# An attention and feed-forward kernel: order of the first loads, weight products side by side, and the place of h1's copies

## Chip, core and metric

The kernel runs on one core of a Trainium2 chip, in float32 (with matmuls in a reduced 32-bit form, written as a high and a low part). The metric is the device time of one execution in microseconds. The median of three runs before the change is 877.68 us (877.13 to 878.19).

## What is computed

The input x has two sequences of 2048 rows and 256 features. The reference, cut to what matters:

```python
xn = _layernorm(x, axis=-1)
q, k, v = xn @ Wq, xn @ Wk, xn @ Wv
attn = softmax(causal(q @ k.T) * 256 ** -0.5)
a = (attn @ v) @ Wo
h = silu((xn @ w1.T) * w1_s) * ((xn @ w2.T) * w2_s)
h = gelu((h @ h1.T) * h1_s)
h = gelu((h @ h2.T) * h2_s)
out = x + a + (h @ w3.T) * w3_s
```

The hidden width is 1024, and w1, w2, h1, h2 and w3 hold only −1, 0 and 1.

## The kernel before

There are two stages. The first, some 280 us, is attention; the second is the feed-forward part (FFN), which begins only when the first has ended and a flag has been read.

**Attention.** Rows are taken in eight blocks of 512 (four to a sequence), each of four tiles of 128 rows. Two algebraic steps shorten the work: Wq and Wk are multiplied into one matrix `wqk`, and Wv and Wo into `wvo`, both by `weights_product` (L217), which makes a high part and a low part of each product. So the keys are just the transposed, normalised x. `keys(n)` (L293) takes one block: `start_keys` (L275) computes mean and variance on VectorE (DVE; `stats`, L235), the root on ScalarE (ACT) and its reciprocal on DVE (`root`, L241), and normalises four tiles on GpSimd (POOL, L283). TensorE (PE) transposes the result (L309), and `hi_lo` (L212) copies it out: the high part on ACT (L214), the low part on DVE (L215). `queries` (L313) multiplies keys by `wqk`, six matmuls of 512 columns for each half; `values` (L327) multiplies keys by `wvo`, 24 matmuls of 256 columns for a block; `score` (L349) multiplies queries by keys. Every such product is a sum of three terms, high by high, high by low and low by high. Softmax exponentials are on ACT (L385). Most of the exponential blocks are transposed through DRAM: DVE turns 32 by 32 squares (L255), one DMA writes them (`d<-b`, L260) and four read them back rearranged (`e<-d`, L267); ACT and DVE or POOL then make the high and low parts `pT` (L423, L425), and `weigh` (L434) multiplies them by the values.

**Beside it.** The kernel chooses a short FFN if all weights are whole, small numbers. It looks at every weight for that: `items` lists pieces of weights of 512 KB or twice 512 KB, which are fetched into `stg` tiles (`fetched_weights`, L577, on ACT's DMA queue) and looked at by DVE, ACT and POOL. w1 and w2 are also rounded into their tiles on the way (`item_low`, L548). For h1, sums of its quarters are written to DRAM (`item_factors`, L554; sums at L150, stored at L541), and three plain quarters are copied from DRAM to DRAM (`copy_factors`, L543): 12 DMAs of 256 KB in all. A planner (`beside`, L600) counts matmul columns and takes the next step of this list, `looks`, when its gap is reached, from the fourth tile on.

**What sets the order.** The program text gives priorities; a scheduler that simulates the engines places each instruction on its engine in the order in which it becomes ready, unless it is tied. `tc.issue_after(ins)` ties what the block issues on that instruction's engine to come after it; it adds no wait. `marks["DVE"]` and `marks["ACT"]` are the latest score scan and the latest exponential. DMAs are started by the instruction queues of SyncE (SP) and of ACT. A DMA that depends on nothing may be placed at the very beginning, and so the h1 copies are: all 12 start between 1.7 and 19.9 us.

**The start.** x's last block of the first sequence is loaded on SP in two halves (L180), Wq and Wk on ACT's queue (L187), then the other blocks on SP. 14 matmuls of zeros (L210) run meanwhile. Wv and Wo are loaded (L611) into the same two tiles after Wq and Wk have been used, and their product stands in the program after the first score. The lines that order it are L608 to L622.

Of the kernel before, what the change touches and what calls it, by code (L numbers as in the profile page):

```python
# [20 lines left out]
P = 128  # L21
TB = 512
# [12 lines left out]
WARM = 14  # L35
# [27 lines left out]
def attn_ffn_kernel(  # L63
# [58 lines left out]
    HK = HC // 2  # L122
    factors = {k: dram.tile([P, len(STEPS), HK, HB], F32, name=f"factors_{k}") for k in ("h1", "h2")}

# [33 lines left out]
    with ExitStack() as actx:  # L158
# [15 lines left out]
        xs, rstds, ks, qs, vs = {}, {}, {}, {}, {}  # L174

        def load_x(n):
            t = xp.tile([P, NT, D], F32, tag="x", name=f"x_{n}")
            for h in range(2):
                src = x[n // NB, ds((n % NB) * TB + h * 2 * P, 2 * P), :]
                nc.sync.dma_start(out=t[:, ts(h, 2), :], in_=src.rearrange("(t p) d -> p t d", p=P))  # L180
            return t

        xs[NB - 1] = load_x(NB - 1)
        raw = {}
        for name, src in (("q", wqT), ("k", wkT)):
            raw[name] = stgp.tile([P, DC, D], F32, tag="stg", name=f"raw_{name}")
            nc.scalar.dma_start(out=raw[name], in_=src)  # L187
        nc.scalar.preload_act_table(AF.Sqrt)
        for n in range(NB - 2, -1, -1):
            xs[n] = load_x(n)  # L190
# [15 lines left out]
        idle = sp.tile([P, S], F32, tag="s", name="idle")[:, : TB // 2].bitcast(BF16)  # L206
        nc.vector.memset(idle, 0.0)
        ps_idle = ps_s.tile([P, TB], F32, tag="ps", name="ps_idle")
        for _ in range(WARM):
            nc.tensor.matmul(out=ps_idle, lhsT=idle[:, :P], rhs=idle, start=True, stop=True)  # L210

        def hi_lo(hi, lo, src):  # L212

            nc.scalar.copy(hi, src)  # L214
            nc.vector.tensor_tensor(lo, src, hi.bitcast(F32), ALU.subtract)  # L215

        def weights_product(name, aT, b, factor):  # L217

            r = cp.tile([P, DC, 2, D], F32R, name=name)
            for c in range(DC):  # L220
                ps = ps_s.tile([P, TB], F32, tag="ps", name=f"ps_{name}_{c}")
                for d in range(DC):
                    nc.tensor.matmul(
                        out=ps[:, :D], lhsT=aT[:, d, ts(c, P)], rhs=b[:, d, :],
                        start=(d == 0), stop=(d == DC - 1),
                    )
                f = rp.tile([P, D], F32, tag="y", name=f"wf_{name}_{c}")
                nc.scalar.mul(f, ps[:, :D], factor)
                nc.vector.tensor_copy(r[:, c, 0, :], f)
                nc.vector.tensor_tensor(  # L230
                    r[:, c, 1, :], f, r[:, c, 0, :].bitcast(F32), ALU.subtract
                )
            return r
# [41 lines left out]
        def start_keys(n):  # L275
            xt = xs.pop(n)
            if n not in rstds:
                mv = cp.tile([P, NT, 2], F32, name=f"mv_{n}")
                stats(xt, mv, n)
                rstds[n] = root(mv, NT, str(n))  # L280
            rstd, off = rstds[n]
            for t in range(NT):
                nc.gpsimd.tensor_scalar(  # L283
# [817 lines left out]
```

## Time and profile before

| what | value |
|---|---|
| median of three runs | 877.68 us |
| the profiled execution | 877.43 us |
| its span | 875.6 us |
| keys, scores and values of the first sequence: last matmul before PE's next wait | ends at 38.68 us |
| first matmul of the FFN (L741) | 279.72 us |
| h1 copies (L544, L546), from issue to landing, least / median / greatest | 3.6 / 5.8 / 7.0 us |
| statistics, DVE L238 and L239, one of each | 0.414 and 0.165 us |
| high part ACT L214, low part DVE L215, 512 columns | 0.587 and about 0.69 us |

The span runs from the first instruction to the last; the rest of the profiled execution, 1.8 us, lies around it. In the lines that follow, PE is the matmul and PEld the loading of its weights. PE's durations overlap, so its pace is read from the time that a group of them takes. A bracket at the end of a line gives the idle time of the engine before it and what ended it. The granted clock (PEclk) is a share of full speed.

### The profile page before, as it was taken

The page shows a single profiled execution, that of the slowest core. Times are in us where ns is not written, and L with a number is a line of the kernel's source. Part 1 is how long each engine was busy: PE and PEld are TensorE (multiplying, and loading weights), DVE is VectorE, ACT ScalarE, POOL GpSimd, SP SyncE. Part 2 cuts the span into 40 slices and gives each one's busy share as a digit, 9 for nine tenths or more (in the row PEclk, how much of TensorE's full clock was granted, in tenths as well). Part 3 has the DMA queues.
Part 4 walks back from the last instruction along what each step waited for, and adds up shares of the span by engine and source line. Part 5 has one row for each costly group of instructions (what it writes and reads, how often), then busy time and mean ns, then how long its engine had stood idle before and what let it go on. Part 6 is the DMA issues. An engine that isn't in the chain of part 4 may idle for free.

```text
span 875.6 us, 12225 instructions
## 1 busy us (share of the span) xinstructions
PE 854.3 (98%) x4280; PEld 721.6 (82%) x4280; DVE 630.6 (72%) x1127; ACT 498.0 (57%) x881; POOL 235.6 (27%) x176
## 2 busy tenths in 40 slices
PE   8999999999998999999999999999999999999996
PEld 5888878988877877888988888888888898888886
DVE  5698689796873995985496596569468648848663
ACT  2546555754753664677266586536557635657670
POOL 4012533202121574440143050025024012502401
PEclk8999999999999999999999999999999999999998
DMA  8877599866892969744424444432434442144312
GB/s 305 326 229 242 168 321 293 302 236 200 238 325 91 365 239 378 258 147 145 139 90 146 147 144 145 156 125 99 144 144 145 147 142 97 49 144 145 144 49 77
DMA packets 63989, 162.51 MB, mean 186 GB/s; under 512 B 6704, under 2 KB 36528, under 8 KB 54704
## 3 DMA queue, kind: packets, MB, share of 16 engines
q1 hardware_dynamic: 58448, 145.92, 48.6%
q10 hardware_dynamic: 5472, 15.73, 5.6%
q8 instruction: 36, 0.59, 0.3%
q14 instruction: 33, 0.27, 0.1%
HBM read 117.06 MB, written 47.71 MB: 188 GB/s over the span
## 4 chain that ended last, share of the span: by engine, by line
PE 70%; DMA 13%; DVE 7%; issue 2%; ACT 2%; SPq 2%; POOL 2%; ACTq 0%; DVEq 0%; POOLq 0%
PE ps_h_X L789 26%; PE ps_w_B L741 13%; PE ps_h_Z L789 13%; PE ps_h_Y L789 7%; PE ps_y L897 6%; DMA e<-d 6%; DMA d<-b 4%; DMA stg<-in_ffn_h_w 2%; SPq L267 2%; DVE b L255 2%; PE pv L336 1%; PE po L443 1%; DVE stg L530 1%; POOL x L283 1%; DVE s L373 1%
## 5 line engine op out<-in xcount | busy, mean ns | idle before, releaser
L364 PE MATMUL pss<-k,q 128*128 128x512 f32 (+3 forms) x480 | 111.0, 369 | 3.1 <-DVE q L215 1.7
L364 PEld LDWEIGHTS pss<-k,q 128*128 128x128 f32 x480 | 81.8, 189 | 16.2 <-DVE q L215 2.1
L789 PE MATMUL ps_h_X<-h_h_T,w_h_S 128*128 128x512 f32 x384 | 89.0, 389 | 0.0
L789 PEld LDWEIGHTS ps_h_X<-h_h_T,w_h_S 128*128 128x128 f32 x384 | 72.1, 188 | 15.0
L443 PE MATMUL po<-v,pT 128*128 128x512 f32 x272 | 79.7, 405 | 3.0 <-ACT pT L423 1.9
L425 POOL TENSOR_TENSOR pT<-e,pT 128x512 fp32r<-128x512 f32 (+3 forms) x30 | 36.3, 1212 | 162.3 <-ACT pT L423 101.6
L887 POOL TENSOR_TENSOR rt<-rt,xt 128x1024 f32<-128x1024 f32 x8 | 19.7, 2458 | 216.5 <-DMA rt<-r_d 200.3
L810 ACT ACTIVATE k_h_u<-k_h_u,h_s_sb 128x512 f32<-128x512 f32 x64 | 46.1, 722 | 41.6 <-DVE k_h_u L809 41.4
L746 ACT ACTIVATE f_w_B<-ps_w_B,w_s_sb 128x512 f32<-128x512 f32 x64 | 42.8, 683 | 43.1 <-PE ps_w_B L741 43.1
L741 PE MATMUL ps_w_B<-xh,w_sb 128*128 128x512 f32 x256 | 60.0, 391 | 2.9 <-DVE f_w_B L747 1.6
L897 PEld LDWEIGHTS ps_y<-w_sbt,h_h_B 128*128 128x128 f32 x512 | 62.0, 192 | 0.3
L897 PE MATMUL ps_y<-w_sbt,h_h_B 128*128 128x256 f32 x512 | 62.1, 283 | 0.0
L423 ACT CAST pT<-e 128x512 fp32r<-128x512 f32 (+3 forms) x60 | 32.6, 573 | 49.6 <-DMA e<-d 38.3
L741 PE MATMUL ps_w_B<-xh1t,w_sb 128*128 128x512 f32 x256 | 60.6, 396 | 0.0
L789 PE MATMUL ps_h_Y<-h_h_B,w_h_A 128*128 128x512 f32 x256 | 59.3, 389 | 0.0
L789 PE MATMUL ps_h_X<-h_h_T,w_h_A 128*128 128x512 f32 x256 | 59.3, 389 | 0.0
L741 PEld LDWEIGHTS ps_w_B<-xh,w_sb 128*128 128x128 f32 x256 | 47.7, 188 | 13.4 <-DVE f_w_B L747 2.0
L443 PEld LDWEIGHTS po<-v,pT 128*128 128x128 f32 x272 | 49.0, 193 | 11.0 <-ACT pT L423 2.4
L741 PEld LDWEIGHTS ps_w_B<-xh1t,w_sb 128*128 128x128 f32 x256 | 48.1, 188 | 11.8
L789 PEld LDWEIGHTS ps_h_Y<-h_h_B,w_h_A 128*128 128x128 f32 x256 | 48.0, 188 | 10.0
L789 PEld LDWEIGHTS ps_h_X<-h_h_T,w_h_A 128*128 128x128 f32 x256 | 48.0, 188 | 10.0
L385 ACT ACTIVATE s<-s,low 128x1024 f32<-128x1024 f32 (+7 forms) x48 | 43.0, 898 | 21.3 <-DVE low L379 21.0
(139 smaller groups left out, 1845.3 us busy)
## 6 DMA issues: line engine op xcount, KB each, us to landing
w_h_S<-factors_h SPq DMA_DIRECT2D x32, 1024.0 KB, 4.7
w_h_A<-factors_h SPq DMA_DIRECT2D x24, 1024.0 KB, 4.7
d<-b SPq DMA_DIRECT2D x18, 512.0 KB, 4.3
e<-d SPq DMA_DIRECT2D x72, 128.0 KB, 4.1
xT_d<-k SPq DMA_DIRECT2D x8, 1024.0 KB, 8.7
stg<-in_ffn_h_w ACTq DMA_DIRECT2D x16, 512.0 KB, 6.5
x<-in_attn_x SPq DMA_DIRECT2D x16, 256.0 KB, 6.5
r_d<-r SPq DMA_DIRECT2D x8, 512.0 KB, 5.5
```

Of the source, the lines that this page charges most:

```text
L255: nc.vector.transpose(b.rearrange("p (g k q) -> p k g q", g=P // Q, q=Q), src.rearrange("p (k g q) -> p k g q", g=P // Q, q=Q),)
L364: nc.tensor.matmul(out=ps[:, :w], lhsT=qs[n][:, c, a, ts(t, P)], rhs=ks[m][:, c, b, :w], start=(k == 0), stop=(m < n and k == 3 * DC - 1),)
L385: marks["ACT"] = nc.scalar.activation(st["s"][:, at], st["s"][:, at], AF.Exp, bias=low, accum_out=st["sums"][:, u // UK : u // UK + 1],).ins
L423: nc.scalar.copy(hi, src)
L425: engine.tensor_tensor(lo, src, hi.bitcast(F32), ALU.subtract)
L443: nc.tensor.matmul(out=st["po"], lhsT=pT[:, 0, ts(j, P)], rhs=vs[m][:, j, :, :], start=(m == first and j == 0), stop=False,)
L741: nc.tensor.matmul(out=p, lhsT=w[:, c, ts(o, P)], rhs=xh[:, c, a, :], start=(c == 0 and a == 0), stop=(c == DC - 1 and a == 1),)
L746: nc.scalar.activation(f, p1, AF.Silu, scale=sc["w1"][:, o : o + 1])
L789: nc.tensor.matmul(out=out[o], lhsT=w[:, c, ts(o, P)], rhs=sets[right][c][:, a, :], start=(start and c == 0 and a == 0), stop=(c == HK - 1 ...
L810: nc.scalar.activation(C[k][o], r[o] if r else banks[o], AF.Gelu, scale=s[:, at : at + 1])
L887: nc.gpsimd.tensor_tensor(rest, rest, xt, ALU.add)
L897: nc.tensor.matmul(out=ys[t][:, :D], lhsT=h[c][:, a, ts(t, P)], rhs=w3_sb[:, c, :], start=(c == 0 and a == 0), stop=(c == HC - 1 and a == 1),)
```

## The change

Its parts:

- x's last block goes out first, one half on SP and one on ACT; then Wq and Wv on SP, Wk and Wo on ACT. Wv and Wo have a tile of their own (from the pool of the turned blocks), so they no longer wait for Wq and Wk. The other x blocks follow on SP.
- `weights_product` makes both halves of a product in one PSUM tile and returns a function that copies them out, 512 columns to an instruction. The product of Wv and Wo stands right after that of Wq and Wk; its copies come after the high and low parts of the first queries.
- The first block's xn is made by POOL (tiles 0 and 2) and ACT (tiles 1 and 3). The statistics of the three next blocks stand behind the low part of `wqk` on DVE.
- The idle matmuls are 26 of 256 columns instead of 14 of 512, and six more follow the first keys.
- In `queries` and `score` the terms are ordered by kind (high by high for both chunks, then low by high, then high by low) instead of by chunk.
- The h1 copies are steps of the w1 and w2 items, 5,000 columns after the look at each, no longer the last step of h1's items; they, and the fetches of the weights that are looked at, are placed behind the latest exponential on ACT.

```diff
-WARM = 14
+WARM = 26
+WARM_KEYS = 6
...
-        def load_x(n):
+        def load_x(n, queues):
             t = xp.tile([P, NT, D], F32, tag="x", name=f"x_{n}")
-            for h in range(2):
+            for h, queue in enumerate(queues):
...
-                nc.sync.dma_start(out=t[:, ts(h, 2), :], in_=src.rearrange("(t p) d -> p t d", p=P))
+                queue.dma_start(out=t[:, ts(h, 2), :], in_=src.rearrange("(t p) d -> p t d", p=P))
...
-        xs[NB - 1] = load_x(NB - 1)
-        raw = {}
-        for name, src in (("q", wqT), ("k", wkT)):
-            raw[name] = stgp.tile([P, DC, D], F32, tag="stg", name=f"raw_{name}")
-            nc.scalar.dma_start(out=raw[name], in_=src)
+        xs[NB - 1] = load_x(NB - 1, (nc.sync, nc.scalar))
+        raw = {name: stgp.tile([P, DC, D], F32, tag="stg", name=f"raw_{name}") for name in "qk"}
+        both = bp.tile([P, 2, DC, D], F32, tag="b", name="raw_vo")
+        raw["v"], raw["o"] = both[:, 0], both[:, 1]
+        for name, src, queue in (
+            ("q", wqT, nc.sync), ("k", wkT, nc.scalar), ("v", wvT, nc.sync), ("o", wo, nc.scalar)
+        ):
+            queue.dma_start(out=raw[name], in_=src)
         nc.scalar.preload_act_table(AF.Sqrt)
         for n in range(NB - 2, -1, -1):
-            xs[n] = load_x(n)
+            xs[n] = load_x(n, (nc.sync, nc.sync))
...
+        def keep_warm(k):
+            for _ in range(k):
+                nc.tensor.matmul(
+                    out=ps_idle[:, : TB // 2], lhsT=idle[:, :P], rhs=idle[:, : TB // 2], start=True, stop=True
+                )
+
+        keep_warm(WARM)
...
+            ps = ps_s.tile([P, DC, D], F32, tag="ps", name=f"ps_{name}")
             for c in range(DC):
-                ps = ps_s.tile([P, TB], F32, tag="ps", name=f"ps_{name}_{c}")
                 for d in range(DC):
...
-                        out=ps[:, :D], lhsT=aT[:, d, ts(c, P)], rhs=b[:, d, :],
+                        out=ps[:, c, :], lhsT=aT[:, d, ts(c, P)], rhs=b[:, d, :],
...
+            def copied():
+                f = rp.tile([P, NT, D], F32, tag="r", name=f"wf_{name}")[:, :DC, :]
+                nc.scalar.mul(f, ps, factor)
+                nc.vector.tensor_copy(r[:, :, 0, :], f)
+                marks["lo"] = nc.vector.tensor_tensor(
+                    r[:, :, 1, :], f, r[:, :, 0, :].bitcast(F32), ALU.subtract
+                ).ins
+
+            return r, copied
...
-                stats(xt, mv, n)
+                with ExitStack() as behind:
+                    if n < NB - 1:
+                        behind.enter_context(tc.issue_after(first_lo))
+                    stats(xt, mv, n)
...
+                if n == NB - 1 and t % 2:
+                    nc.scalar.activation(
+                        xt[:, t, :], xt[:, t, :], AF.Identity,
+                        scale=rstd[:, t : t + 1], bias=off[:, t : t + 1],
+                    )
+                    continue
...
-            for c in range(DC):
-                for a, b in ((0, 0), (0, 1), (1, 0)):
+            for a, b in ((0, 0), (1, 0), (0, 1)):
+                for c in range(DC):
...
         def copy_factors(src, f, c):
-            nc.scalar.dma_start(out=f[:, 0, c, :], in_=src[:, c, :HB])
-            for i in range(2):
-                nc.scalar.dma_start(out=f[:, 5 + i, c, :], in_=src[:, c + HK, ts(i, HB)])
...
+            with tc.issue_after(marks["ACT"]):
+                nc.scalar.dma_start(out=f[:, 0, c, :], in_=src[:, c, :HB])
+                for i in range(2):
+                    nc.scalar.dma_start(out=f[:, 5 + i, c, :], in_=src[:, c + HK, ts(i, HB)])
...
-                (3000, lambda t: copy_factors(src, f, c)),
...
+            copy = (5000, lambda t, c=c: copy_factors(h1, factors["h1"], c))
+            item_low(src[:, c % DC, :], dst[:, c % DC, :], (copy,))
...
-                nc.scalar.dma_start(out=t, in_=src)
+                with tc.issue_after(marks["ACT"]):
+                    nc.scalar.dma_start(out=t, in_=src)
...
-        wqk = weights_product("wqk", raw["q"], raw["k"], scale)
-        for name, src in (("v", wvT), ("o", wo)):
-            raw[name] = stgp.tile([P, DC, D], F32, tag="stg", name=f"raw_{name}")
-            nc.scalar.dma_start(out=raw[name], in_=src)
+        wqk, wqk_copied = weights_product("wqk", raw["q"], raw["k"], scale)
+        wvo, wvo_copied = weights_product("wvo", raw["v"], raw["o"], 1.0)
         keys(NB - 1)
+        wqk_copied()
+        first_lo = marks["lo"]
+        keep_warm(WARM_KEYS)
         queries(NB - 1, 0)
         queries(NB - 1, 1)
         order = list(range(NB - 1, -1, -1))
         score(NB - 1, NT - 1, NB - 1, order)
-        wvo = weights_product("wvo", raw["v"], raw["o"], 1.0)
+        with tc.issue_after(marks["hi"]), tc.issue_after(marks["lo"]):
+            wvo_copied()
```

(`hi_lo` sets `marks["hi"]` and `marks["lo"]` to its last two instructions.) Unchanged: the DMAs of the transposed blocks, all of the FFN, and the amount of arithmetic, the idle matmuls apart.

## The prediction

> **What bounds the kernel now.** I read the page first, for the busy shares; then the busy times by short stretches over the first 40 us; then what TensorE (PE) waited for; then the order of work there; then the chain of waits. The page, parts 1 and 2:
>
> ```profile
> span 875.6 us, 12225 instructions
> ...
> PE 854.3 (98%) x4280; PEld 721.6 (82%) x4280; DVE 630.6 (72%) x1127; ACT 498.0 (57%) x881; POOL 235.6 (27%) x176
> ...
> PEclk8999999999999999999999999999999999999998
> ```
>
> PE is busy 98%, and the one low clock digit before the end is the first. So TensorE's work is the bound, and what can be won is what it loses, most of it in the first slice. The stretches of the start (PE, PEld, DVE, ACT, POOL busy; then PE clock, DMA share, GB/s):
>
> ```profile
> 4.00:8.00 4.00, 3.73 (x16) 2.02 (x14) 2.39 (x10) 0.30 (x1) 0.00 (x0) 1.00 1.07 388
> 8.00:12.00 4.00, 2.00 (x8) 0.89 (x8) 3.58 (x18) 1.05 (x3) 2.29 (x4) 0.86 1.07 385
> 12.00:16.00 4.00, 3.75 (x8) 2.66 (x9) 3.54 (x14) 1.18 (x4) 1.15 (x3) 0.50 0.97 321
> 16.00:20.00 4.00, 4.00 (x19) 3.23 (x18) 2.12 (x10) 1.44 (x3) 3.57 (x7) 0.79 0.88 252
> ...
> 28.00:32.00 4.00, 4.00 (x33) 3.82 (x32) 2.46 (x6) 1.69 (x3) 1.57 (x2) 1.00 1.04 406
> ```
>
> From 8 to 12 us PE has half a load of small transposes; from 12 to 16 it is "busy" with 8 matmuls at half clock; by 28 to 32 it runs 33 at full clock. The cause in order of time (start, length, engine, line, tiles):
>
> ```profile
> 5.78 1.97 PE L223 MATMUL ps_wqk<-raw_k,raw_q 128*128 128x256 f32 x8
> 6.26 0.76 DVE L238 BATCH_NORM_STATS2 st<-x 128x6 f32<-128x256 f32 x2 [0.47 <-DMA x<-in_attn_x]
> 7.34 0.30 ACT L243 ACTIVATE std<-mv,eps 128x4 f32<-128x4 f32 x1 [4.38 <-DVE mv L239]
> 7.55 0.75 DVE L238 BATCH_NORM_STATS2 st<-x 128x6 f32<-128x256 f32 x2 [0.32 <-DMA x<-in_attn_x]
> 8.30 0.14 DVE L245 RECIPROCAL rstd<-std 128x4 f32<-128x4 f32 x1
> 8.75 2.29 POOL L283 TENSOR_SCALAR x<-x,rstd,off 128x256 f32<-128x256 f32 x4 [6.50 <-DVE off L247]
> 11.10 0.69 PE L309 MATMUL ptx<-ident,x 128*128 128x128 f32 x2 [0.22 <-POOL x L283]
> 12.25 5.62 PE L320 MATMUL pq<-k,wqk 128*128 128x512 f32 x12 [0.46 <-ACT k L214]
> ...
> 18.61 1.02 PE L223 MATMUL ps_wvo<-raw_o,raw_v 128*128 128x256 f32 x4
> ```
>
> The chain of waits agrees, and shows the full-clock price of the same matmul shape far away:
>
> ```profile
> 8.75 2.30 POOL x L283 x4
> ...
> 12.25 5.62 PE pq L320 x12
> ...
> 348.37 7.25 PE ps_h_Y L789 x32
> ```
>
> 12 matmuls took 5.62 us (0.47 each) where 32 later took 7.25 (0.227 each). After 17.87 the chain is PE almost without a break to 38.68. From 280 us on (FFN) PE loses nearly nothing; that part touches none of the edits and stays.
>
> **What the Trainium skill says.** "TensorE: Matmul & The Clock Gate", Part 1, states that an idle window of about 3.4 us drops the array to half clock and a busy one restores it, on a window that runs freely. The trace agrees: PE thins out from 7.75 us and the 12-to-16 stretch has a granted clock of 0.50. "DMA: Bandwidth & Descriptors", Issuing engines are not separate DMA queues, says transfers from several issuers share the same 16 engines and a second issuer saves only issue time. The DMA share is already 1.07 at 388 GB/s with two queues, so only the order of bytes can win, not the second queue. "ScalarE: Activation LUTs", Table sets, says cheap functions such as identity sit in every set, so the new Identity instructions need no table load beside Sqrt; the trace has no Identity, but copies run after Sqrt here without a load.
>
> **The change part by part.** All times are positions in the span; the profiled execution took 877.43 us, 0.25 below the median of 877.68.
>
> *Order of the loads.* Today x's first half comes at 4.80 (chain), the second at 6.26, since Wq, Wk and the first h1 copies go out on ACT's queue beside it. Afterwards x's two halves go first, one on each queue. 512 KB and then 1 MB of four weights at about 388 KB a us: I put x at 4.7, Wk at 5.9 (today PE begins the product at 5.75) and Wo at 7.2. The h1 copies (12 DMAs, 3 MB) leave these 20 us, so the other x blocks come earlier (the last is waited for until 15.22 today), though Wq and Wv now stand ahead of them on SP's queue: two issues of under 0.5 us and 1.3 us of transfer, hidden since the held statistics ask for them only at about 10.
>
> *Statistics.* Two tiles take 0.97 us of DVE (4.83 to 5.80), four take 1.94: done at 6.65, std 0.30 more. Today rstd then waits 0.66 us because DVE has gone to the next block's statistics; the new order holds those behind wqk's low part. rstd and off take 0.35: POOL starts at about 7.4 instead of 8.75.
>
> *xn by two engines.* Four POOL instructions are 2.29; two are 1.15. ACT's two cost about 0.38 each (L228, same width). The last xn is ready at about 8.6 instead of 11.04. ACT may have to place wqk's 0.6 us multiply in between; that is inside the same time.
>
> *Products side by side.* wqk is 8 records in 1.73 us, wvo as much: 5.95 to 9.4 on PE, so the transposes stand behind them or between them. Behind: 8 transposes at 0.11 bring the last pair to 9.95; between: 8.6. Today 1.15 us pass from the last pair (11.10) to the queries (12.25). So queries start between 9.75 and 11.1; I take 10.4, a gain of 1.85. The weight copies merge 2+2+2 instructions of 256 columns into one of 512 each, on ACT and DVE: fixed costs of some tenths, hidden.
>
> *Clock.* The 26 idle matmuls have half the columns of the 14 before: about the same 4 us of cover at the front, then 3.5 us of products, then transposes, six more fillers (about 0.11 each, 0.65 in all, in a hole). No gap nears 3.4 us, so I expect full clock: 12 × 0.227 = 2.72 instead of 5.62. The new order of terms uses k's low part last; it ends about 1.65 us after the first matmul today, while 4 matmuls cover 0.9, so 0.6 us of wait stays. Queries end at 10.4 + 2.72 + 0.6 = 13.7 instead of 17.87: 4.15 gained.
>
> *wvo off the later path.* Its two groups of 0.87 us in the chain at 18.77 and 20.56 go: 1.73 gained. Its copies wait behind q's on ACT and DVE, and the next keys' copies queue behind them; that is in the holes below.
>
> *What is late next.* After the queries the score needs q's high and low parts, 0.6 and 0.7 us; transposes and wvo filled that hole before. Block 2's statistics (2.3 us), roots, 2.3 us of POOL and transposes now begin only at about 10, so keys(2) come near 16 to 17; the score (1.4) and values(3) (2.8) cover until then, once wvo's copies are through DVE. From 10 us DVE has three blocks of statistics (12 × 0.58 = 7.0), 8 k low parts (5.4), 7 v and 2 q (6.2), wvo (1.6), 4 scores (2.8), wqk's remains and roots (1): 24 us, which ends at 34, just where PE would be. I price these holes at 2.0 us (bounds 0.7 and 4).
>
> Sum: 4.15 + 1.73 − 2.0 = 3.9 us.
>
> *h1 copies and fetches, held.* The 12 copies now follow the four w1/w2 items on ACT's queue, behind an exponential each. By the planner's counts (gaps in matmul columns) the first comes 6,000 columns after the first low pass, which is at 71.64 us on ACT today (L523), and the last 63,000 later, where h1's first sums are now (104.78, L150): about 74 to 103 us. Each costs ACT about 0.5 us of issue: 6.6 us where ACT is 11.81 of 20 busy (80 to 100), so it fits; queued behind them on ACT are the exponentials and pT's high parts. 3 MB at some 390 KB a us, read and written, is about 8 us of all DMA engines where the share is 0.57: it fits in the mean, but can delay a block's return. Held fetches still come before their use: four steps of 4,000 to 8,000 columns, some 11 us by the planner for one-tile items, against 5.5 to 6.5 us to land. The four 5,000s added and four 3,000s removed shift the middle items by some 8 us; the last look stays in the last tile, so the flag is not later. I take 0 for all this; bounds −4 (better) and +8.
>
> **The rivals.** *DVE becomes the start's bound*: the deferred statistics cost the full 4 us of holes; gain 1.9, 875.5. For: 24 us in 24 us. Against: v's last low parts aren't needed at once. *Handed back later*: near 122 to 130 us block returns took over 9 us to land at a DMA share of 0.99; PE idled 2.15 us between 100 and 150 and had one 3.4 us window at half clock (1.7 lost). One more such stall costs 3.9: 877.4, no change. *Such a stall disappears* because the items shift: 869.6. *Slower*: the h1 copies between 74 and 103 us meet the returns of the transposed blocks, which ACT's and DVE's pT parts wait for (10.8 us for ACT between 40 and 120 already, all covered by PE's lead of two blocks). If a return grows from 4.1 us past that lead, each block pays; two such stalls of 3.9 cost 7.8 against 3.9 gained: 881.3. It decides once more than 5.7 us of PE idleness appear after 40 us. *The change does not do what it says*: the clock window falls badly and the queries still run at half clock; gain 1.0, 876.4.
>
> **How the numbers follow.** Likeliest (0.55): 877.43 − 3.9 = 873.5, own range 871 to 875.3. DVE-bound 0.12, handed back 0.10, clock not held 0.04, stall gone 0.10, slower 0.09. A measurement of this kernel tells about 0.2% (1.75 us) from no change, so faster means below 875.9: 0.55 + 0.10 + most of DVE-bound (0.10) = 0.75. Same: 0.10 + 0.04, with the slow edges of the others, less the fast edges = 0.14. Slower: 0.09 and a tail of the handed-back case = 0.11. The range takes in the stall that goes (869.3) and ends at the case handed back (877.4).
>
> **What would show it.** Right: x's four xn by about 8.6, queries in under 3.5 us from about 10.4, granted clock 1.00 from 8 to 16, no L223 after 12, the end of the key and value phase near 35 instead of 38.7, and the FFN beginning about 4 us before 279.7. Wrong: a clock of 0.5 in the queries; PE waiting for DVE or POOL between 14 and 34; waits of PE for pT between 60 and 130 that are not there now; or an FFN start that has not moved.

## The result and the profile after

The changed kernel takes 881.67 us (879.76 to 883.52, five runs) beside 877.68 (877.13 to 879.11, five runs) before: 1.0043 times as long, 95% interval 1.0028 to 1.0059. It is slower, by 0.43%; 873.5 us had been predicted.

The start is faster, as it was meant to be. The page of the changed kernel first, then PE's busy time in the stretches of the start (columns as before), then single instructions of the start:

```profile
span 878.0 us, 12255 instructions
...
PE 851.8 (97%) x4298; PEld 720.9 (82%) x4298; DVE 626.5 (71%) x1123; ACT 499.4 (57%) x881; POOL 235.9 (27%) x174
...
PEclk9999999999999999999999999999999999999998
```

```profile
4.00:8.00 4.00, 4.00 (x29) 3.51 (x28) 2.03 (x10) 1.50 (x4) 1.09 (x2) 1.00 1.06 381
8.00:12.00 4.00, 3.54 (x21) 2.79 (x20) 3.44 (x12) 1.66 (x4) 0.00 (x0) 1.00 1.05 287
12.00:16.00 4.00, 3.55 (x14) 2.07 (x13) 4.00 (x17) 1.95 (x5) 1.43 (x3) 1.00 0.87 328
...
80.00:120.00 40.00, 36.28 (x195) 30.15 (x195) 30.30 (x67) 22.63 (x43) 20.94 (x25) 1.00 0.96 298
```

```profile
6.67 1.09 ACT L303 ACTIVATE x<-x,off,rstd 128x256 f32<-128x256 f32 x2 [0.44 <-DVE off L263]
6.74 1.09 POOL L308 TENSOR_SCALAR x<-x,rstd,off 128x256 f32<-128x256 f32 x2 [4.49 <-DVE off L263]
...
7.69 1.89 PE L236 MATMUL ps_wvo<-raw_vo 128*128 128x256 f32 x8
...
9.42 1.04 PE L334 MATMUL ptx<-ident,x 128*128 128x128 f32 x8
...
10.91 3.29 PE L345 MATMUL pq<-k,wqk 128*128 128x512 f32 x12 [0.46 <-ACT k L227]
```

The first xn is made by two engines side by side, PE has no hole from 4 us to 10.46, the granted clock is 1.00 from 4 to 16 us, and the twelve query matmuls take 3.29 us instead of 5.62.

One part did not come out as written. The six idle matmuls that follow the first keys in the program were placed by the scheduler at the very front with the other 26, so PE runs all 32 before the first product. Here is after, then e8, the same kernel run once more:

```profile
1.05 5.01 PE L219 MATMUL ps_idle<-idle 128*128 128x256 bf16 x32 [1.05 <-DVE idle L214]
...
5.91 1.95 PE L236 MATMUL ps_wqk<-raw_k,raw_q 128*128 128x256 f32 x8
```

```profile
1.06 6.60 PE L219 MATMUL ps_idle<-idle 128*128 128x256 bf16 x32 [1.06 <-DVE idle L214]
...
7.49 1.89 PE L236 MATMUL ps_wqk<-raw_k,raw_q 128*128 128x256 f32 x8
```

In after, the pace of the idle matmuls doubles at about 3.9 us (0.21 us each, then 0.11), and they end about when Wk lands (5.75). In e8 it doubles only at about 7.1 us; Wk had landed at 5.98, and the product waited 1.5 us behind them. In eight of ten profiles with the new start and the copies held or moved the product starts at 6.7 to 7.5. The first xn is ready at 7.83 (8.05 in e8), while its transposes stand behind both products, at 9.42 (10.95).

The last line of the second fence above is the other half of the story: from 80 to 120 us PE is busy 36.28 of 40. Before, the same stretch read:

```profile
80.00:120.00 40.00, 40.00 (x217) 34.17 (x216) 30.48 (x68) 23.91 (x47) 21.32 (x26) 1.00 0.78 235
```

What PE waited for ACT's pT in the whole run, in the view of PE's waits (us in all, times, longest), first before, then after:

```profile
PE po L443 <- ACT pT L423: 1.9, 1, 1.9
```

```profile
PE po L467 <- ACT pT L447: 9.5, 9, 3.3
```

And the end of the kernel, in the chain of waits, before:

```profile
862.18 3.41 DMA rt<-r_d
...
868.64 1.72 DMA out<-yt
```

After, with the place ahead of it where this chain leaves the matmuls of the first values:

```profile
34.09 1.07 PE pv L361 x9
...
861.86 4.41 DMA rt<-r_d
...
869.31 3.19 DMA out<-yt
```

A few landmarks of the two profiled executions (877.43 and 879.76 us) put the account together:

| landmark, us | before | after | difference |
|---|---|---|---|
| twelve query matmuls end | 17.87 | 14.20 | −3.67 |
| last values matmul of the first sequence starts | 39.79 | 36.28 | −3.51 |
| first matmul of the FFN | 279.72 | 279.27 | −0.45 |
| last matmul starts | 868.26 | 867.93 | −0.33 |
| span | 875.6 | 878.0 | +2.4 |

(The 38.68 us of the first table is where the chain of waits leaves the values, 35.16 now; it is not their end, and PE does not wait there. The last of them ends at 40.07 before and 36.56 after.)

So 3.5 us are won in the start, 3.1 are handed back in the attention stage, the FFN's matmuls take as long as before, and the tail, where a residual load and the stores of the output land later, costs 2.7 more. This is one pair of executions, and after's was the shortest of its five. In e8 the last values matmul starts at 37.68, attention gives back 4.9 us, and the FFN takes 1.6 us longer too. Over ten profiles with the new start (copies held or moved) and seven with the old one the last values matmul starts at 36.6 and 39.6 us in the mean: the start gains about 3.0.

### The profile page after: what moved, and what is told of

Its sections match the earlier page's. It is cut to its first block, busy times and chain, and to the rows that moved or that the text cites. A ratio compares the mean times of both kernels' runs of the same rounds, so it can differ in the third digit from the quotient of the medians.

```text
span 878.0 us, 12255 instructions
## 1 busy us (share of the span) xinstructions
PE 851.8 (97%) x4298; PEld 720.9 (82%) x4298; DVE 626.5 (71%) x1123; ACT 499.4 (57%) x881; POOL 235.9 (27%) x174
## 4 chain that ended last, share of the span: by engine, by line
PE 76%; DMA 11%; DVE 5%; ACT 3%; issue 2%; POOL 1%; SPq 1%; ACTq 0%; DVEq 0%; POOLq 0%
PE ps_h_X L817 26%; PE ps_h_Z L817 13%; PE ps_w_B L769 13%; PE ps_h_Y L817 7%; DMA e<-d 6%; PE ps_y L925 6%; PE pss L388 3%; PE po L467 3%; DMA stg<-in_ffn_h_w 2%; PE pv L361 2%; PE pq L345 1%; DVE b L271 1%; PE po L472 1%; DVE s L397 1%; DMA d<-b 1%
## 5 line engine op out<-in xcount | busy, mean ns | idle before, releaser
L774 ACT ACTIVATE f_w_B<-ps_w_B,w_s_sb 128x512 f32<-128x512 f32 x64 | 42.9, 683 | 42.4 <-PE ps_w_B L769 42.4
L795 POOL TENSOR_TENSOR k_h_u<-k_h_p,k_h_u 128x512 f32<-128x512 f32 x16 | 24.3, 1523 | 111.9 <-ACT h_h_B L752 99.4
```

The lines of the kernel that those rows point to most:

```text
L774: nc.scalar.activation(f, p1, AF.Silu, scale=sc["w1"][:, o : o + 1])
L795: nc.gpsimd.tensor_tensor(B["B12"][i], B["B22"][i], B["B12"][i], ALU.subtract)
```

## The experiments

They ran on more than one chip, so each ratio is to the runs of before on its own chip. One reading is used throughout: the *loss* of PE in a stretch is the time from each matmul's start to the next one's, less its price at full clock (0.227 us for 512 columns), summed. From 80 to 120 us it is 2.2 before and 7.1 after. The last three columns of this table are from one profiled execution each. *Attention* runs from the start of the last values matmul to the start of the FFN, so it leaves the start out; *tail* runs from the start of the last matmul to the end of the span. After and e8 are the same program and differ by 1.9 us of attention, so smaller differences between two single profiles say little.

| kernel | ratio to before, interval | last values matmul | attention | tail |
|---|---|---|---|---|
| before | | 39.8 | 239.9 | 7.4 |
| after | 1.0043 (1.0028 to 1.0059) | 36.3 | 243.0 | 10.1 |
| e8_changed_again | 1.0056 (1.0036 to 1.0077) | 37.7 | 244.9 | 10.9 |
| e1_start_alone | 1.0106 (1.0074 to 1.0138) | 42.3 | 248.9 | 10.6 |
| e2_copies_free | 1.0144 (1.0119 to 1.0170) | 39.5 | 249.8 | 8.2 |
| e3_fetches_free | 1.0120 (1.0092 to 1.0149) | 42.4 | 250.2 | 8.4 |
| e4_held_alone | 1.0055 (1.0033 to 1.0078) | 39.4 | 248.7 | 7.9 |
| e5_copies_in_lull | 1.0035 (1.0021 to 1.0049) | 37.0 | 244.3 | 10.1 |
| e6_four_more_idle | 1.0044 (1.0028 to 1.0061) | 40.3 | 247.6 | 7.8 |
| e7_term_order | 1.0079 (1.0048 to 1.0111) | 39.1 | 248.7 | 8.2 |
| g1_exponentials_first | 1.0125 (1.0098 to 1.0153) | 37.7 | 250.6 | 10.1 |
| g2_longer_lead | 1.0125 (1.0103 to 1.0147) | 37.0 | 253.0 | 10.1 |
| g3_old_term_order | 1.0070 (1.0057 to 1.0083) | 35.4 | 247.3 | 10.8 |
| g4_one_idle_less | 1.0051 (1.0033 to 1.0069) | 38.6 | 244.5 | 7.9 |
| k1_idle_order_of_before | 0.9984 (0.9970 to 0.9997) | 39.9 | 240.6 | 8.0 |
| k2_before_order_of_idle | 1.0046 (1.0025 to 1.0068) | 40.3 | 246.2 | 7.7 |
| k3_start_order_of_before | 1.0074 (1.0045 to 1.0103) | 36.2 | 245.1 | 8.3 |
| k4_start_free_order | 1.0034 (1.0017 to 1.0051) | 36.0 | 244.9 | 10.0 |
| k5_late_copies_order | 0.9990 (0.9971 to 1.0010) | 36.3 | 239.3 | 11.2 |
| k6_late_copies_free | 1.0064 (1.0044 to 1.0084) | 36.7 | 243.3 | 10.1 |

### Is it the held copies and fetches?

**e1_start_alone** is the changed kernel with copies and fetches as before (the copies again the last step of h1's items); e2_copies_free takes away only the first of these ties, e3_fetches_free only the second.

```diff
-            with tc.issue_after(marks["ACT"]):
-                nc.scalar.dma_start(out=f[:, 0, c, :], in_=src[:, c, :HB])
+            nc.scalar.dma_start(out=f[:, 0, c, :], in_=src[:, c, :HB])
...
-                with tc.issue_after(marks["ACT"]):
-                    nc.scalar.dma_start(out=t, in_=src)
+                nc.scalar.dma_start(out=t, in_=src)
```

> The changed kernel with its start kept, but h1's copies and the weight fetches as in the kernel before: copies are again the last step of h1's items and nothing is placed behind an exponential. Theory A (the start wins about 3.5 us and the held copies and fetches lose it again in the attention stage and more): 873 to 875 us, FFN beginning near 276 us. Rival B (the start's gain is swallowed by the attention stage whatever the copies do, because something else paces it): 877 to 880 us, FFN near 279. Rival C (the copies return to the first 20 us and slow the start itself): the queries end after 15 us instead of 13.8 and the time is 876 to 878.

> The changed kernel with one tie removed: h1's copies are not placed behind an exponential (their place in the list stays), so all 12 can go out at the start; the fetches stay held. If the copies on ACT's queue cost the time (theory A, copies): 874 to 877 us, and PE's wait for ACT's pT falls from 9.5 us to about 4. If the held fetches cost it (theory A, fetches): about 881, as the changed kernel. Rival B: 878 to 881.

> The changed kernel with the other tie removed: the weight fetches are not placed behind an exponential, the copies stay held. If the copies cost the time: about 880 to 882 us and PE's wait for ACT's pT stays near 9 us. If the fetches cost it: 875 to 877. Rival B: 878 to 881.

All three are slower than the changed kernel, at 889.9 to 892.6 us beside a before of 880.1, above every case written down. The start itself is spoilt: the last values matmul comes at 39.5 to 42.4 instead of 36.3. Rival C had that mechanism, far too small. The timeline of ACT, its queue and PE in e1 shows how (a bracket is the engine's idle time and what ended it; ACTq is ACT issuing a DMA):

```profile
8.65 0.55 ACTq L570 DMA_DIRECT2D factors_h<-in_ffn_h_w  x1
9.25 0.60 ACT L243 ACTIVATE wf_wqk<-ps_wqk 128x512 f32<-128x512 f32 x1 [1.24 <-DMA factors_h<-in_ffn_h_w]
...
12.27 1.07 ACT L227 CAST k<-ptx 128x512 fp32r<-128x512 f32 x2 [2.42 <-DMA factors_h<-in_ffn_h_w]
...
17.51 0.30 ACT L259 ACTIVATE std<-mv,eps 128x4 f32<-128x4 f32 x1 [4.17 <-DMA stg<-in_ffn_w_w]
...
19.47 0.80 PE L388 MATMUL pss<-k,q 128*128 128x512 f32 x1 [3.49 <-ACT q L227]
```

ACT reads nothing of h1, and yet its copies of wqk and k and its root are let go by landings of h1 copies and fetches. The compiled program says why. Every DMA of SP and of ACT counts up one of eight semaphores, and its issue waits until the previous DMA on that one has landed:

```
7  L570 DMACopy factors_h_69<-in_ffn_h_w 128x512 [waits DMAHW1_49]
10 L570 DMACopy factors_h_69<-in_ffn_h_w 128x512 [waits DMAHW3_49]
14 L604 DMACopy stg_0_717<-in_ffn_w_w 128x1024 [waits DMAHW2_49,DMAHW1_49]
```

With eight in flight, the ninth issue stands in ACT's instruction stream and all of ACT's work behind it. In e1's first 24 us ACT idled 8.9 us so. The Trainium skill, "DMA: Bandwidth & Descriptors", Why a DMA increments its semaphore by 16 and not by 1, asks for one semaphore for each DMA in flight; here that is eight, shared by both issuers. So holding both the copies and the fetches is what lets the start gain at all.

**e4_held_alone** is the reverse: the kernel before with only the copies and fetches held as in the change.

> The kernel before with only the second half of the change: copies as steps of the w1 and w2 items, copies and fetches placed behind the latest exponential; the start as before, free of the copies. Theory A: the loss without the gain, 882 to 886 us. Rival B (the start decides nothing and the held copies cost nothing either): 877 to 879.

Its start is as before, its attention 8.7 us longer, and PE waited 12.4 us for ACT's pT, nine times. This alone would put the loss on the copies and fetches; but the edit also changes the order of the other instructions. **e5_copies_in_lull** takes them out of their new place: they go on SP behind the last store of the keys, from about 31 us, where the transfers idle.

```diff
-            with tc.issue_after(marks["ACT"]):
-                nc.scalar.dma_start(out=f[:, 0, c, :], in_=src[:, c, :HB])
+            with tc.issue_after(marks["xT"]):
+                nc.sync.dma_start(out=f[:, 0, c, :], in_=src[:, c, :HB])
```

> The changed kernel with h1's 12 copies moved: no longer steps between 69 and 90 us on ACT's queue, but issued on SP's queue right behind the last store of the first sequence's keys (30.6 us in the changed kernel), where the DMA share falls to 0.00. Fetches stay held. If the held copies cost what the start won (theory A): PE loses about 2 to 3 us less between 80 and 120 us, the FFN begins near 276 and the time is 876 to 878. If it is the attention stage's order that was fitted to the old start (theory B): PE still loses 6 us or more between 80 and 120, and the time is 880 to 890.

The loss from 80 to 120 falls to 5.3 us (8.2 in e8, the changed kernel again, on the same chip), but from 140 to 200 it grows to 8.9 (5.5 in e8). So the loss lies between the two theories, the time is B's. The intervals of e5 and e8 overlap, and before is still faster.

> The changed kernel once more, on the chip of these runs. Its profile says whether the losses between 80 and 120 us and the late output at the end come again (then they belong to the kernel) or move (then they are chance). Theory A and B: 1.003 to 1.006 of before, FFN beginning at 279 to 283 us.

e8 waits for pT at the same places as the first profile of after (2.39 us at 103.99 there, 2.46 at 105.60 in e8, whose start is later by 1.4): the loss belongs to the kernel, not to one execution.

### Does anything leave the attention stage alone?

Two edits to the kernel before that touch no copy: **e6_four_more_idle** (`WARM = 18`) and **e7_term_order** (the order of terms in queries and score; in score the two low terms stand the other way round than in the change). On another chip, **g4_one_idle_less** (`WARM = 13`).

```diff
-WARM = 14
+WARM = 18
```

```diff
-            for c in range(DC):
-                for a, b in ((0, 0), (0, 1), (1, 0)):
+            for a, b in ((0, 0), (1, 0), (0, 1)):
+                for c in range(DC):
```

> The kernel before with 18 idle matmuls instead of 14 at the start and nothing else: about 0.9 us more of idle work before the first product, which the wait for xn hides. Theory B (every shift of the start makes the scheduler choose other orders in the attention stage, and the order of before is a lucky or fitted one): slower by 4 us or more, with the loss after 40 us. Theory A (only the moved DMAs cost): within 1.5 us of before.

> The kernel before with the new order of terms in the queries and scores alone. Theory B: slower by 4 us or more, since it moves instructions on DVE and ACT. Theory A: within 1.5 us of before, or up to 0.5 us faster at the first queries.

> The kernel before with 13 idle matmuls instead of 14, nothing else. Theory 'any order but before's loses': slower than before by 0.2 to 0.8%, with new waits of PE for pT between 80 and 140 us, although its start is not later than before's. Rival 'what counts is that the start is later': four idle matmuls more cost 0.44%, so one less costs nothing or gains, ratio 0.999 to 1.000.

All three are slower than before, by 0.4 to 0.8%, with attention 4.5 to 8.8 us longer; g4's start was not even later. For the idle matmuls nothing in the edit itself costs that; the order of terms is looked at below. What they share is that the scheduler, whose simulated times they shift, orders the attention stage otherwise: e6's program has 15 matmuls, 5 ACT, 13 DVE, 1 POOL and 4 SP instructions of that stage elsewhere.

Two attempts to mend the changed kernel by its wait for pT failed. **g1_exponentials_first** ties each cast of pT behind the latest exponential, **g2_longer_lead** sets `DELAY_BLOCKS = 48000`. **g3_old_term_order** puts the terms back, which moves 8 DVE and 2 ACT instructions beside the matmuls themselves.

```diff
-                nc.scalar.copy(hi, src)
+                with tc.issue_after(marks["ACT"]):
+                    nc.scalar.copy(hi, src)
```

```diff
-DELAY_BLOCKS = 42000
+DELAY_BLOCKS = 48000
```

> The changed kernel with one tie more: in the turning of a block, the ACT copy that makes pT's high part is placed behind the latest exponential on ACT. Nothing else differs, and nothing is added to do. Theory 'casts ahead of exponentials': in the changed kernel a cast that waits for a late block return stands ahead of exponentials and so delays the next block too; with the tie PE's waits for ACT's pT fall from 9.5 to 10.1 us to under 5, the FFN begins at 276 to 278 us, and the time is 0.3 to 0.5% below the changed kernel's, about 878. Rival 'any order but before's loses': the loss moves to another place, and the time is 0.4 to 1% above before. A third, 'the cast then comes too late': PE's waits for pT grow above 12 us and the time goes above 886.

> The changed kernel with DELAY_BLOCKS 48000 instead of 42000: a row's weighing stands 6,000 matmul columns (about 2.7 us of PE) later behind its scores. Theory 'returns outlast PE's lead': PE's waits for ACT's pT fall from about 10 us to under 5, the FFN begins by 277 us or earlier, and the time falls to 877 to 880. Rival 'any order but before's loses': the order changes too, the loss between 60 and 260 us stays at 6 us or more above before's, and the time is 0.4 to 1% above before.

> The changed kernel with the terms of queries and score ordered by chunk again, as before the change; the order of DVE and ACT stays nearly the same as in the changed kernel. Theory 'any order but before's loses': the term order costs nothing by itself (it cost 0.79% alone in the kernel before only because it changed the rest of the order), so the time is the changed kernel's within 0.2%, ratio to before 1.003 to 1.006, with the same waits for pT near 90 and 103 us. Rival 'the term order costs by itself': 3 us or more faster than the changed kernel, ratio about 1.000, the gain spread evenly over the queries and scores.

g1 and g2 changed the order widely and lost 1.25%, more than any case but g1's third had put; in g1 PE still waited 10.6 us for pT, and g2's extra lead, which should have covered the waits, ended with PE waiting 13.0 us for pT. g3, with nearly the same order as the changed kernel, is no faster than it (1.0070 beside e8's 1.0056): the 0.79% of e7 were not the terms' own.

### The order by itself

In all of these an edit and an order change together. The next two part them. After the attention stage, ties are added that put each engine's instructions, from the first exponential on, into a listed order (the list is read off another program); nothing else differs.

```diff
+        traced = {i.name: i for i in nc.cur_bb.bb.instructions}
+        for listed in ORDER.values():
+            names = [n for n in ("I-" + k for k in listed.split(",")) if n in traced]
+            for a, b in zip(names, names[1:]):
+                tc.add_manual_dep(
+                    traced[b], a,
+                    mybir.DependencyInfo(mybir.DependencyClass.NoSync, mybir.DependencyReason.DATA),
+                    reason="order",
+                )
```

**k1** is e6's kernel with the order of before; **k2** is the kernel before with e6's order.

> The kernel before with 18 idle matmuls instead of 14 (it measured 1.0044 times before), now with the instructions of the attention stage (from the first exponential on) tied on each engine into the order that they have in the kernel before; without the ties 15 matmuls, 5 ACT, 13 DVE, 1 POOL and 4 SP instructions of that stage stand elsewhere. Theory 'the order decides': as fast as before, ratio 0.998 to 1.0015, the FFN begins within 1.5 us of its place in a run of before. Rival 'the shift in time decides': still 1.003 to 1.006.

> The kernel before itself, its 14 idle matmuls and its start untouched, with the attention stage tied into the order that it has with 18 idle matmuls: the same few instructions stand elsewhere. Theory 'the order decides': 1.003 to 1.006 times before, with waits of PE for pT or for s between 80 and 140 us. Rival 'the shift in time decides': ratio 0.998 to 1.0015.

k1 is as fast as before although its start is e6's, k2 as slow as e6 although its start is before's. Over 80 to 140 us, k1 and then k2:

```profile
80.00:140.00 60.00, 58.19 (x329) 50.26 (x329) 45.60 (x107) 34.47 (x68) 24.23 (x29) 1.00 0.88 261
```

```profile
80.00:140.00 60.00, 55.13 (x285) 45.68 (x284) 40.87 (x95) 32.45 (x63) 23.74 (x28) 0.97 0.81 238
```

The DMA share is lower in the slow one, so it isn't a want of bandwidth. The timelines show the links (SPq is SP issuing DMAs). In k1:

```profile
69.50 0.13 DVE L488 TENSOR_REDUCE low<-tops 128x1 f32<-128x3 f32 x1
...
72.72 1.24 DVE L364 STREAM_TRANSPOSE b<-s 128x1024 f32<-128x1024 f32 x1
...
74.55 2.51 SPq L376 DMA_DIRECT2D e<-d  x4
...
80.12 0.62 ACT L532 CAST pT<-e 128x512 fp32r<-128x512 f32 x1
...
80.69 1.15 ACT L494 ACTIVATE s<-s,low 128x1024 f32<-128x1024 f32 x1
...
90.83 0.62 ACT L532 CAST pT<-e 128x512 fp32r<-128x512 f32 x1 [1.25 <-DMA e<-d]
```

The same instructions in k2, with two that stand ahead of them there:

```profile
70.80 0.69 DVE L630 TENSOR_SCALAR stg<-stg 128x1024 uint32<-128x1024 uint32 x1
71.40 0.15 DVE L488 TENSOR_REDUCE low<-tops 128x1 f32<-128x3 f32 x1
...
73.60 1.40 DVE L347 BATCH_NORM_STATS2 st<-x 128x6 f32<-128x256 f32 x4
...
74.92 1.23 DVE L364 STREAM_TRANSPOSE b<-s 128x1024 f32<-128x1024 f32 x1
...
76.63 2.34 SPq L376 DMA_DIRECT2D e<-d  x4
...
84.04 0.62 ACT L532 CAST pT<-e 128x512 fp32r<-128x512 f32 x1 [4.43 <-DMA e<-d]
...
86.10 1.14 ACT L494 ACTIVATE s<-s,low 128x1024 f32<-128x1024 f32 x1
...
95.90 0.62 ACT L532 CAST pT<-e 128x512 fp32r<-128x512 f32 x1 [4.27 <-DMA e<-d]
...
98.62 0.73 PE L473 MATMUL pss<-k,q 128*128 128x512 f32 x2 [0.82 <-DVE s L482]
```

On DVE a look at weights (L630) goes before a row's maximum and statistics (L347) before the turning of its block; in k1 both stand behind. The maximum is 1.9 us late, the turning 2.2. Some 0.5 us of each such difference is older than this: the same instructions stand 0.5 us apart at 60 us already. In SP's queue the store of this block stands ahead of the return of an *earlier* block, so that return is issued 2.1 us late, and it lands later still. ACT's cast of it, 3.9 us late, stands ahead of the exponential of yet another row, whose maximum had been ready since 81.6 (81.45 us plus 0.14); that one starts 5.4 us late (a copy of q, and a look at weights that ran ahead of the cast in k1, stand between the two here, 1.5 us). The cast of the next block returned follows at 95.90 instead of 90.83, and at 98.62 PE waits. Each queue is in order, each waits for another, and so a delay of 1.9 us comes back as 5.

### Can the start's gain be kept?

**k3** gives the changed start the order of before, by the same ties; **k4** is k3 without them. Both have e5's copies and the old term order, so that the lists fit, and hold only the first two fetches:

```diff
-                with tc.issue_after(marks["ACT"]):
+                with ExitStack() as behind:
+                    if i < 2:
+                        behind.enter_context(tc.issue_after(marks["ACT"]))
                     nc.scalar.dma_start(out=t, in_=src)
```

> The changed kernel's start (loads, products side by side, xn by two engines, idle matmuls), with the terms ordered by chunk as before, the h1 copies on SP behind the stores of the keys, the first two fetches held behind an exponential, and the attention stage from the first exponential on tied into the order of the kernel before. Theory 'the order decides': the start's 3.5 us are kept; values end near 36, the FFN begins at 275 to 277.5, PE loses at most 3 us between 80 and 120, and the time is 873 to 876 beside a before of 878, ratio 0.994 to 0.998: faster than both kernels. Rival 'the earlier start meets later returns, whatever the order': PE waits for pT again, the FFN begins at 279 or later, ratio 1.000 to 1.005.

> The kernel of k3_start_order_of_before without the given order: the same start, terms, copies and first fetches, and the scheduler's own order. Theory 'the order decides': ratio 1.003 to 1.008, the FFN at 280 or later. Rival: the same time as k3_start_order_of_before within 0.2%.

Here the rival was right: the old order did not keep the gain, and k4 without it is not slower than k3. k3 lost 2.05 us at 49.57, where before lost nothing. How long the first turned blocks took to land, k3 and then before:

```profile
DMA to landing us min/median/max: 5.9/5.9/5.9
```

```profile
DMA to landing us min/median/max: 2.6/2.8/2.9
```

The h1 copies, issued from 31.3 to 40.9 us and landing until 46.8, ran beside these stores. **k5** therefore moves them behind the last block return (near 262 us, where the transfers idle) and the two fetches back to the values, about 30 us, and keeps the list; **k6** is k5 without it.

```diff
-        for c in range(HK):
-            copy_factors(h1, factors["h1"], c)
+        last_hi = marks["hi"]
...
-            with tc.issue_after(marks["xT"]):
+            with tc.issue_after(marks["e"]):
...
+        for c in range(HK):
+            copy_factors(h1, factors["h1"], c)
```

> The changed kernel's start with the terms ordered by chunk; the 12 h1 copies on SP behind the last block return of the attention stage (about 262 to 265 us), the first two fetches behind the high parts of the values (about 30 us), and the attention stage tied into the order of the kernel before. Theory 'order and transfers together': with both as before from 38 us on, the start's gain is kept: values end near 36, nothing lost at 49.6, PE loses under 3 us between 80 and 120, the FFN begins at 275.5 to 277.5, time 873.5 to 876, ratio 0.993 to 0.998. Rival 'an order fits one timing': the same order, 3.5 us earlier, meets other landings and waits for pT again; the FFN begins at 279 or later, ratio 0.999 to 1.006.

> As k5_late_copies_order, with the scheduler's own order. Theory 'order and transfers together': 0.3 to 0.8% above before, at least 0.5% above k5_late_copies_order. Rival 'transfers alone': at or below before, the same as k5_late_copies_order.

In k5 the gain reaches the FFN, which begins at 275.67, 4.05 us before before's. PE's wait for pT and its busy time from 80 to 140 us (k5, then before) are near those of before:

```profile
PE po L578 <- ACT pT L558: 2.9, 2, 2.7
```

```profile
80.00:140.00 60.00, 58.41 (x340) 51.07 (x339) 46.10 (x103) 33.76 (x67) 25.64 (x30) 1.00 0.87 265
```

```profile
80.00:140.00 60.00, 57.85 (x311) 49.44 (x310) 45.10 (x105) 33.74 (x67) 23.89 (x28) 0.97 0.86 255
```

k6, the same work in the scheduler's own order, is slower by 0.7% than k5 (1.0064 against 0.9990, intervals apart). Yet k5's time, 876.66 us beside 877.87, cannot be told from before's. Its last matmul starts 3.75 us earlier, at 864.51, and its span is 875.7, before's own: the tail takes 11.2 us instead of 7.4. Its chain of waits ends like after's:

```profile
858.44 4.48 DMA rt<-r_d
...
865.95 3.08 DMA out<-yt
```

So k5 beats the changed kernel and only equals the one before. What makes the tail longer is open: it is 7.4 to 8.2 us in the seven kernels with the old start and 10.0 to 11.2 in ten of the thirteen profiles with the new one, but 8.2 to 8.4 in e2, e3 and k3. Fetches of instructions run through the same transfers in these last microseconds, before and after; that they are what the stores wait for was not tried.

## Why the prediction was wrong

**The start: right, though the way there was not all as forecast.** xn was ready at 7.83 (8.6 predicted), the queries started at 10.91 (10.4), took 3.29 us (2.72 + 0.6) at full clock, and ended at 14.20 (13.7): 3.67 us gained of the 4.15. The Trainium skill, "TensorE: Matmul & The Clock Gate", Part 1, which the clock term rested on, held: once full at 3.9 us, the clock did not fall to half before 263 us in this execution. wvo's 1.73 us are off the later path. The holes that take their place follow from the sum, 3.67 + 1.73 − 3.51 = 1.9, where 2.0 was put. At the last values matmul 3.5 of 3.9 us stood, about 3.0 in the mean of the profiles, and the rival with DVE as the bound fell. Of the two cases, transposes between the products or behind them, the later one came (its last pair belongs at 9.4 + 6 × 0.11 = 10.06, not at 9.95), and the six fillers priced in a hole stood at the front, where all 32 together kept the first product waiting in eight of ten profiles. That they ended just as Wk landed in the profiled execution was luck.

**"I take 0 for all this": the step that failed.** The place of copies and fetches was priced at nothing with bounds of −4 and +8. Alone, with the order that it brought about, it cost 0.55% (e4), some 4.8 us, within the bounds and far from the value taken. The argument made for 0 was about capacity: ACT's issue time fits in, 8 us of transfers fit into a share of 0.57. The transfers were priced too low. In k3 the copies took 15.5 us on a nearly idle stretch. In after, where the share from 80 to 120 rose from 0.78 to 0.96, block returns issued from 75 to 110 us took 5.2 us to land in the mean (5.1 in e8) instead of 4.0. But capacity is not all of it: k2 loses 0.46% with returns of 3.9 us in that stretch and a lower DMA share than k1, by the places of some 40 instructions.

**The step that wasn't written down.** The sum ended at 38 us, and "873.5" needs the attention stage to pass the gain on unchanged. It did not: 3.1 us came back there in the profiled execution (4.9 in e8), and attention was longer in every other kernel whose order was left to the scheduler (243.0 to 253.0 against 239.9). Only the two with both the order of before and transfers much as before, k1 and k5, kept its length (240.6 and 239.3). How much of the changed kernel's own 3.1 us is the transfers' and how much the order's stays open: with the copies taken away (e5) the loss above before's from 80 to 120 us was 3.1 instead of e8's 6.0, and k6, with returns as short as before's (3.6 us), still lost by its order. The text counted cause and effect per instruction, but an edit in the start also reorders work far behind it.

**The tail.** No term stood for it, since the FFN "touches none of the edits and stays". Its matmuls did stay; its last transfers took 2.7 us more, which alone makes the difference between no change and slower in the profiled execution.

**The rivals.** The slower one, copies that meet block returns, gave 881.3, near the measured 881.67, but was only partly the reason: e5 took the copies away from there and kept half of the loss between 80 and 120 us and most of the time. "Handed back later" had the late returns and the sign; the place that it looked at, 122 to 130 us, was wrong, and its size, one stall, too small. "Such a stall disappears" came as well and was outweighed: from 120 to 160 us after loses 4.6 us and before 7.1, and before's half clock at 126.9 us is gone. Both signs listed as "wrong" came: waits of PE for pT, and an FFN start that hardly moved. The range (869.3 to 877.4) left out 881.3, which had a chance of 0.09. A chance that any reordering costs the order that had been found was not among the cases.

**The second queue.** The skill's sentence that several issuers save only issue time ("DMA: Bandwidth & Descriptors", Issuing engines are not separate DMA queues) was used to say that the second queue wins nothing. e1 to e3 show that it can lose: an issue that waits for a landing stops ACT's arithmetic.

## What to carry to other kernels

Where a scheduler orders the instructions, an edit has two effects, its own and that of the order it brings about: compare the two orders beyond the edit before giving a gain at one place to the whole kernel, and fix the order to measure the edit alone. In in-order queues, look for an instruction that waits for a transfer and stands ahead of one that starts the next, and for work that could wait ahead of one that can't. Here a DMA issued from an engine that also computes cost only its issue (0.5 us on ACT in e1) while fewer than eight were in flight, and stopped that engine otherwise. And look up in the timeline where filler work was placed: its place in the program text does not tell.

## What the runs showed beyond that

- Four idle matmuls more, or one less, at the very start of the kernel cost 0.44% (0.28 to 0.61) and 0.51% (0.33 to 0.69), and for the four more, the order of before gave it all back (k1, 0.9984).
- SP and ACT together never had more than eight DMAs in flight in the profiles counted (before, after, e1, k3); in e1 issues began 0.01 to 0.02 us after the landing that they waited for (7.24 after 7.23, 8.84 after 8.82, 11.12 after 11.10).
- Twelve DRAM-to-DRAM copies of 256 KB on a nearly idle stretch took from 31.3 to 46.8 us (k3), some 200 GB/s counted once, and the stores among them took 5.9 us instead of 2.8.
- The end of a program can differ by 3 us with the same work in it: from the last matmul's start to the end, k3 took 8.3 and k4 10.0, which differ only in the ties on the attention stage, 590 us earlier.
